# A new table of keys for the order of all steps in a convolution, Fourier and FFN kernel

## The chip, the cores and the metric

The kernel runs on one core of a Trainium2 chip, as one launch over 64 images. The metric is device time in microseconds: the median of three runs before is 7462.52 us (7462.07 to 7469.69). A core has five engines that run their own instruction queues: TensorE (PE; its weight loads are shown as PEld), VectorE (DVE), ScalarE (ACT), GpSimd (POOL) and SyncE (SP), which here issues DMAs.

## The reference

Two layers act on a tensor of 64 x 96 x 56 x 56 float32.

- Layer 0 is a convolution block: a 1x1 expansion from 96 to 192 channels with a batch norm and SiLU, a shift of four channel groups by one pixel each, a channel shuffle, a depthwise 3x3 with an identity branch and SiLU, a squeeze-and-excite gate, a 1x1 projection back to 96 channels, the residual, and SiLU.
- Layer 1 takes the 3136 pixels as tokens t of 96 channels.

```
t = t + attn(ln(t))   # ln: mean and variance over the 96 channels
t = t + ffn(ln(t))
# attn: h = relu(bn1(t @ w1.T)), 192 channels; X = fft over the 3136 tokens
#       xr = relu(Xr*rd - Xi*id + rb), xi = relu(Xi*rd + Xr*id + ib)
#       y = real(ifft(xr + i*xi)); bn2(y @ w2.T)
# ffn:  two linear layers 96 -> 384 -> 96, products rounded to fp8 (5 exponent bits),
#       sums and biases rounded to fp16, relu between
```

## The kernel before

**Work and tiles.** One image is one unit of work. It passes through 56 kinds of step, and each kind runs once to 21 times an image. A step is a small function with the arguments b (image) and i (which one), and it issues instructions to a single engine, apart from sp_ev, which also issues a DMA on SP. Names ending in _mm are TensorE's. The steps in the order of an image's data:

- x_in loads 8 rows of x (SP); ea_mm, eb_mm (PE, lines 383 and 400) expand; ea_ev, eb_ev (ACT) apply SiLU.
- dw_mm (L446) computes 128 of the 192 channels of the depthwise convolution on PE in two halves of three steps; lt (L466, L468) computes the other 64 on DVE. dw_ev (L456) and ls apply SiLU on ACT and give the sums for the gate.
- se1_mm (L478), se1_ev, se2_mm (L493), se2_ev, se2_th and se2_pw make the gate and fold it into the projection's weights.
- pj_mm (L532, L537), pj_add (DVE) and pj_ev (ACT) project, add x and write the tokens t.
- c_mm (L557), c_sq, c_v, c_pow (POOL) get the variance of each token; sp_v, sp_mm and sp_ev carry it to where w1 needs it: sp_ev writes a row of t by DMA.
- w1_mm (L626) and w1_ev; then the Fourier transform in two stages, f1_mm (L653) with f1_ev (L665, ACT) and f2_mm (L680, L690); f2_u (L705, ACT), f2_s (L721, L724, DVE), f2_r (L728, ACT) and f2_p (L734, DVE) do the complex scaling with its relu.
- w2_mm (L745, L757), w2_ev; the inverse transform i1_mm (L786), i1_ev, i2_mm (L808), i2_ev.
- n_mm, n_sq, n_v, n_pow, n_x, x_mm (L852), x_ev: the second layer norm, rounded to fp8.
- h_mm (L865), h_ev (L870, ACT), h_b (L875, DVE), h_q (L881, ACT): the first FFN layer, three h to one o; o_mm (L887), o_ev (L892), o_b (L897), o_f (L903, POOL) and o_st (SP): the second, the residual and the store.

**Order.** Nothing is reordered by a scheduler. A table PLAN gives each step a key relative to its image, PERIOD is added for each image, and all steps of all images are issued in the order of these sums:

```
with tc.manual_schedule():
    for _, b, k, i in sorted(
        (b * PERIOD + when, b, k, i)
        for b in range(NB)
        for k, step in enumerate(STEPS)
        for i, when in enumerate(PLAN[step.__name__])
    ):
        STEPS[k](b, i)
```

Each engine then has its part of this list as its own queue. Only the order of the keys matters; they are not times at which something happens. At equal sums the smaller b goes first, then the earlier kind of step. An image's keys reach from about -150 to +310, so in a repeat of one PERIOD the steps of several images interleave: with ea_mm to pj_mm of image b run c_mm to i2_mm of image b-1 (c_mm already of b towards the end), and n_mm to o_mm of image b-2. "Image" numbers in square brackets below are relative in this way.

**Buffers.** PSUM has two kinds here. Two buffers of 1024 columns (psa) are taken in turn by w1_mm, f1_mm, f2_mm, w2_mm, i1_mm and i2_mm: each waits until the step that reads the buffer two turns earlier is done. Four buffers of one bank (psb) serve all other matmuls; a step takes the one that was released first. Both waits, like those for data, are semaphores that the framework puts in. In SBUF the fp16 results of h have three buffers, and the fp8 results, the squares, the scaled spectrum and the outputs two each.

Of the kernel before, what the change touches and what calls it, by code (L numbers as in the profile page):

```python
# [38 lines left out]

PERIOD = 116.056
PLAN = {
    "x_in": (-142.751, -132.334, -138.890, -139.641, -151.208, -133.652, -137.370),
    "ea_mm": (-127.116, -124.446, -119.920, -94.498, -104.745, -112.167, -106.964),
    "ea_ev": (-125.252, -124.279, -119.721, -94.105, -94.974, -110.456, -105.960),
    "eb_mm": (-110.852, -109.364, -102.468, -94.672, -100.705),
    "eb_ev": (-109.889, -108.508, -98.175, -94.671, -100.704),
    "dw_mm": (-77.186, -75.415, -71.686, -59.708, -58.836, -58.630),
    "dw_ev": (-67.184, -68.088, -65.354, -62.005, -53.949, -53.481, -53.376, -53.432),  # L50
    "lt": (-93.236, -91.843, -90.397, -86.333, -83.176, -78.618, -75.060, -71.072, -58.358),
    "ls": (-56.957,),
    "se1_mm": (-52.674,),
    "se1_ev": (-52.590,),
    "se2_mm": (-49.560,),
    "se2_ev": (-47.764,),
    "se2_th": (-46.882,),
    "se2_pw": (-44.842,),
    "pj_mm": (-44.604, -44.263, -36.259, -33.499),
    "pj_add": (-41.623, -41.337, -40.573, -40.255, -32.468, -30.814, -32.509, -32.127),  # L60
    "pj_ev": (-41.036, -40.637, -40.429, -36.736, -30.334, -29.230, -31.146, -29.797),
# [1 line left out]
    "c_sq": (-23.198, -19.663, -17.391, -16.366, -11.963, -8.651, -8.871),
    "c_v": (-21.831, -17.939, -17.390, -11.021, -10.842, -8.366, -8.657),
    "c_pow": (-19.058, -12.292, -10.931, -8.952, -1.526, -3.948, -1.526),
    "sp_v": (-8.951, -1.525),
    "sp_mm": (-6.057, 0.802),
    "sp_ev": (-5.461, 1.113),
    "w1_mm": (1.423, -2.619, 3.588, 18.203, 8.943, 12.171, 13.999, 16.535),
    "w1_ev": (3.273, -0.045, 7.600, 20.920, 11.591, 14.999, 15.957, 19.212),  # L70
# [10 lines left out]
    "i1_ev": (86.931, 93.317, 99.344),
    "i2_mm": (102.107, 101.737, 110.644, 111.766),
    "i2_ev": (106.004, 107.037, 104.651, 104.395, 113.248, 110.645, 115.503, 113.393),
    "n_mm": (109.042, 108.523, 116.336, 120.505, 126.604, 126.539, 137.374),
    "n_sq": (109.105, 109.021, 116.337, 120.506, 127.174, 126.540, 137.375),
    "n_v": (109.642, 109.022, 116.338, 120.507, 127.975, 126.902, 138.122),
    "n_pow": (110.809, 110.170, 116.496, 122.658, 132.126, 129.135, 139.318),
    "n_x": (112.520, 110.693, 119.248, 123.053, 133.298, 130.929, 139.362),
    "x_mm": (113.125, 114.113, 121.321, 126.216, 135.244, 138.382, 142.002),
    "x_ev": (114.896, 115.709, 126.025, 126.217, 137.926, 142.365, 142.302),  # L90
# [1013 lines left out]
```

## Time and profile before

| | |
|---|---|
| median of three runs | 7462.52 us |
| profiled execution, time | 7463.64 us |
| profiled execution, span | 7461.9 us |
| granted TensorE clock | 0.991 |
| PE busy | 7176.9 us, 96% |
| PE weight loads busy | 5259.2 us, 70% |
| DVE busy | 4829.5 us, 65% |
| ACT busy | 4654.4 us, 62% |
| POOL busy | 1513.6 us, 20% |

The profile is of one execution: its span runs from the first to the last instruction, and the time is what the device reports for the same execution. Busy shares are averages. An idle stretch of an engine is listed with what ended it: "PE psa L745 <- DVE ue L724" means that a matmul of line 745, which writes psa, started when the VectorE instruction of line 724, which writes ue, was done. "issue" means that the profile shows nothing that the engine waited for. In a timeline each row is a run of like instructions: start, duration, engine, line, operation, out<-in, shapes and count.

### The profile page before, as it was taken

How to read it: one execution, taken by the hardware profiler on the slowest of the kernel's cores; microseconds unless marked ns; L12 is line 12 of the kernel's file. 1: busy time of each engine (PE TensorE's matmuls, PEld its weight loads, DVE VectorE, ACT ScalarE, POOL GpSimd, SP SyncE). 2: the span in 40 equal slices, each digit the busy share in tenths (PEclk: the TensorE clock that was granted, in tenths of full speed). 3: DMA queues.
4: the chain of work that ended last, by engine and by line, in shares of the span. 5: the costliest groups of instructions: out<-in, count | busy, mean ns of one | idle time of the engine just before them, and what ended most of it. 6: DMA issues, size and time to landing. Idle time of an engine off the chain costs nothing.

```text
span 7461.9 us, 383252 instructions
## 1 busy us (share of the span) xinstructions
PE 7176.9 (96%) x177666; PEld 5259.2 (70%) x177666; DVE 4829.5 (65%) x8795; ACT 4654.4 (62%) x9806; POOL 1513.6 (20%) x1360
## 2 busy tenths in 40 slices
PE   7999999999999999999999999999999999999997
PEld 4777777777777776777777777777777777777775
DVE  5666666666666666666666666666666666666664
ACT  3566666666665666656656666666566566665665
POOL 0221212212212122122121221221212212212112
PEclk9999999999999999999999999999999999999998
DMA  1010110110101101101011011010110110101100
GB/s 48 20 27 18 29 27 19 29 24 21 28 17 29 27 19 28 24 22 28 17 29 27 19 28 25 22 28 18 29 27 19 29 26 20 29 21 26 28 20 21
DMA packets 424331, 185.32 MB, mean 25 GB/s; under 512 B 378785, under 2 KB 422041, under 8 KB 422473
## 3 DMA queue, kind: packets, MB, share of 16 engines
q1 hardware_dynamic: 420970, 155.82, 9.1%
q8 instruction: 1392, 22.81, 1.3%
q10 hardware_dynamic: 1264, 3.48, 0.1%
q14 instruction: 209, 1.71, 0.1%
q0 software_dynamic: 496, 1.50, 0.1%
HBM read 82.80 MB, written 77.07 MB: 21 GB/s over the span
## 4 chain that ended last, share of the span: by engine, by line
PE 85%; ACT 6%; DVE 6%; issue 3%; DMA 0%; POOL 0%; POOLq 0%; SPq 0%; ACTq 0%
PE psa L653 9%; PE psa L626 9%; PE ps_d L446 8%; PE ps_eb L400 5%; PE ps_ea L383 5%; PE psa L808 5%; PE ps_pj L532 5%; PE ps_c L557 5%; PE psa L745 5%; PE ps_n L557 5%; PE psa L786 5%; PE psa L680 4%; PE ps_h L865 4%; PE ps_o L887 3%; DVE s L721 3%
## 5 line engine op out<-in xcount | busy, mean ns | idle before, releaser
L903 POOL TENSOR_TENSOR o<-t,o 112x448 f32<-112x448 f32 x448 | 613.9, 1370 | 3694.7 <-DMA out_dram<-o 1710.0
L446 PE MATMUL ps_d<-e_a,diag 32*32 32x392 f32 x36864 | 1033.2, 498 | 0.7 <-ACT d L456 0.7
L468 DVE SCALAR_TENSOR_TENSOR d_last<-e_b,taps,d_last 128x1568 f32<-128x1568 f32 x512 | 971.5, 1898 | 7.1
L875 DVE TENSOR_SCALAR y<-y,qb 128x448 f16<-128x448 f16 x1344 | 479.8, 365 | 683.9 <-ACT y L870 676.7
L568 DVE TENSOR_REDUCE v<-sq 112x4 f32<-112x384 f32 x896 | 491.3, 548 | 662.7 <-ACT sq L564 662.1
L446 PEld LDWEIGHTS ps_d<-e_a,diag 32*32 32x32 f32 x36864 | 673.6, 103 | 288.9 <-issue 40.0
L870 ACT CAST y<-ps_h 128x448 f16<-128x448 f32 x1344 | 697.2, 540 | 213.1 <-PE ps_h L865 209.5
L837 POOL TENSOR_TENSOR rs<-v,mhalf 112x4 f32<-112x4 f32 x448 | 490.3, 1099 | 1453.9 <-DVE v L569 1453.9
L881 ACT CAST h<-y 128x448 fp8e5<-128x448 f16 x1344 | 739.0, 571 | 3.0 <-DVE y L875 3.0
L653 PEld LDWEIGHTS psa<-f_tab,buf_h 128*56 128x56 f32 x24576 | 655.4, 131 | 77.8 <-DVE v L569 42.5
L626 PEld LDWEIGHTS psa<-w1c,t 112*64 112x64 f32 x14336 | 604.0, 137 | 141.4 <-DVE v L569 45.4
L653 PE MATMUL psa<-f_tab,buf_h 128*56 128x58 f32 x24576 | 688.9, 216 | 0.0
L626 PE MATMUL psa<-w1c,t 112*64 112x96 f32 x14336 | 676.2, 249 | 2.9 <-DMA t<-dev_t 1.4
L586 POOL TENSOR_TENSOR rs<-v,mhalf 112x4 f32<-112x4 f32 x448 | 447.6, 1012 | 763.6 <-DVE v L569 763.5
L638 DVE SCALAR_TENSOR_TENSOR buf_h<-psa,rs_full 128x768 f32<-128x768 f32 (+1 forms) x512 | 435.4, 851 | 137.4 <-PE psa L626 129.5
L543 DVE TENSOR_TENSOR ps_pj<-ps_pj,x 112x392 f32<-112x392 f32 x512 | 260.6, 566 | 404.5 <-PE ps_pj L537 392.3
L728 ACT ACTIVATE s<-s 128x896 f32<-128x896 f32 (+2 forms) x384 | 334.4, 887 | 288.8 <-DVE s L721 288.8
L388 ACT ACTIVATE e_a<-ps_ea 128x448 f32<-128x448 f32 x448 | 244.9, 547 | 412.5 <-PE ps_ea L383 412.5
L564 ACT ACTIVATE sq<-ps_n 112x384 f32<-112x384 f32 x448 | 214.1, 495 | 436.1 <-PE ps_n L557 434.8
L734 DVE SCALAR_TENSOR_TENSOR buf_h<-ue,s 128x448 f32<-128x448 f32 (+2 forms) x768 | 406.8, 580 | 109.4 <-ACT s L728 109.4
L549 ACT ACTIVATE t<-ps_pj,pjbn_b 112x392 f32<-112x392 f32 x512 | 281.4, 620 | 284.5 <-DVE ps_pj L543 284.5
L786 PE MATMUL psa<-inv_tab,buf_g 112*32 112x56 f32 x24576 | 350.5, 214 | 110.5 <-issue 108.8
(175 smaller groups left out, 13024.5 us busy)
## 6 DMA issues: line engine op xcount, KB each, us to landing
x<-in_x SPq DMA_DIRECT2D x896, 84.0 KB, 3.2
out_dram<-o SPq DMA_DIRECT2D x896, 84.0 KB, 2.2
l_tab<-in_tab_l ACTq DMA_DIRECT2D x1, 1624.0 KB
r_tab<-in_tab_r ACTq DMA_DIRECT2D x1, 1568.0 KB
t<-dev_t SPq DMA_DIRECT2D x64, 7.0 KB, 2.1
t<-dev_t SPq DMA_DIRECT2D x64, 5.2 KB
ex_row_p<-in_expand_row POOLq DMA_DIRECT2D x1, 336.0 KB, 4.5
s_p<-in_bn POOLq DMA_DIRECT2D x1, 288.0 KB, 3.8
```

The source lines that it names most:

```text
L446: nc.tensor.matmul(pss[r][j * 32 : j * 32 + 32], lhsT=diag[pr, tap, :], rhs=e_a[pr, r0 : r0 + PJ, dx : dx + HW], start=tap == 0, stop=tap ...
L468: nc.vector.scalar_tensor_tensor(d_last, win, w, d_last, ALU.mult, ALU.add)
L557: nc.tensor.matmul(cen[c0:c1, k, 0:C], lhsT=t_of(b)[:, n0 + c0 : n0 + c1], rhs=center, start=True, stop=True)
L568: nc.vector.tensor_reduce(v, sq, AX.X, ALU.add)
L626: nc.tensor.matmul(ps[hc * 64 : hc * 64 + 64, k, 0:C], lhsT=t[:, n0 : n0 + 64], rhs=w1c[:, hc * C : hc * C + C], start=True, stop=True,)
L653: nc.tensor.matmul(ps[r * 64 : r * 64 + HW, k, 0 : 2 * NK], lhsT=buf_h[:, n0 : n0 + HW], rhs=f_tab[:, r, :], start=True, stop=True,)
L786: nc.tensor.matmul(ps[p0 : p0 + 32, k, 0:HW], lhsT=u_v[:, oh * 48 + o, :], rhs=inv_tab[:, r, :], start=True, stop=True,)
L837: nc.gpsimd.tensor_tensor(rs, held.pop(("nv", b, g)), mhalf[0:CP, 0:4], ALU.pow)
L870: nc.scalar.copy(y16, held.pop(("h", b, i)))
L875: nc.vector.tensor_scalar(y16, y16, qb1[:, i % 3 : i % 3 + 1], 0.0, ALU.add, ALU.max)
L881: nc.scalar.copy(held["h8", b, j][:, m, :], held.pop(("y", b, i)), saturate=False)
L903: nc.gpsimd.tensor_tensor(o32, rows, o16, ALU.add)
```

## The change

PERIOD goes from 116.056 to 116.117, and every key in PLAN is replaced. No function changes, and each kind of step has as many entries as before, so the same instructions are issued in another order. The diff in its core (the other kinds of step have new keys in the same manner):

```diff
-PERIOD = 116.056
+PERIOD = 116.117
 PLAN = {
...
-    "dw_ev": (-67.184, -68.088, -65.354, -62.005, -53.949, -53.481, -53.376, -53.432),
+    "dw_ev": (-75.706, -75.706, -75.706, -75.705, -59.463, -58.046, -59.416, -59.640),
...
-    "c_mm": (-24.403, -20.404, -19.123, -17.297, -18.726, -9.644, -8.872),
+    "c_mm": (-24.700, -23.784, -22.561, -14.383, -22.138, -11.175, -15.521),
...
-    "f1_mm": (21.608, 26.248, 24.638, 31.810, 32.559, 32.004),
-    "f1_ev": (25.169, 25.895, 30.841, 28.844, 27.556, 26.595, 32.009, 32.411, 36.910, 36.732, 36.699, 35.929),
-    "f2_mm": (37.220, 36.994, 44.528, 54.196, 60.721, 63.959),
+    "f1_mm": (20.969, 24.138, 21.453, 27.916, 28.364, 29.033),
+    "f1_ev": (21.858, 21.828, 27.847, 26.717, 25.831, 26.083, 28.752, 28.380, 29.263, 29.263, 29.263, 29.263),
+    "f2_mm": (33.295, 29.847, 41.027, 45.394, 56.500, 57.570),
...
-    "f2_r": (44.699, 46.227, 59.499, 60.966, 71.228, 72.985),
+    "f2_r": (40.411, 40.237, 54.971, 56.273, 70.174, 75.875),
...
-    "i1_mm": (82.811, 83.639, 91.924),
+    "i1_mm": (81.789, 85.039, 89.118),
...
     "h_q": (
-        149.384, 151.139, 150.029, 159.215, 163.340, 163.159, 172.257, 183.329, 182.397, 187.024, 188.763, 189.403,
+        145.380, 145.381, 145.381, 154.154, 164.463, 155.147, 170.447, 186.761, 183.168, 187.741, 191.545, 191.927,
...
-    "o_mm": (153.028, 179.101, 192.712, 203.850, 207.474, 223.800, 230.382),
+    "o_mm": (145.964, 174.332, 192.700, 203.173, 205.203, 221.748, 227.957),
```

What the keys come to, in the queues (the number behind a name is i, the bracket the image relative to b):

| queue, stretch | before | after |
|---|---|---|
| PE, f1 | ea_mm3, f1_mm0[-1], x_mm5[-2], f1_mm2, x_mm6, f1_mm1, h_mm2, 0, 1, 4, f1_mm3, 5, 4, h_mm3, 5, o_mm0, f2_mm1, 0 | f1_mm0[-1], f1_mm2, x_mm5[-2], x_mm6, ea_mm3, f1_mm1, h_mm1, 2, 0, f1_mm3, 4, 5, h_mm5, 3, 4, o_mm0, f2_mm1, 0 |
| ACT, same | ... f1_ev6, 7, h_q0, 2, 1, f1_ev11, 10, 9, 8, h_ev3, 4, o_ev0, h_ev5, f2_u2 | ... f1_ev7, 6, f1_ev8, 9, 10, 11 (h_q0 before or behind these four), h_q1, h_q2, o_ev0, h_ev3, 5, 4, f2_u2 |
| PE, dw to w2 | dw_mm0 to 2, f2_mm2, h_mm6, 8, 7, f2_mm3, dw_mm3 to 5, f2_mm4, h_mm9, o_mm1, se1_mm, f2_mm5, h_mm10, se2_mm, h_mm12, 11, w2_mm0 | dw_mm0 to 2, f2_mm2, h_mm6, 8, f2_mm3, dw_mm3 to 5, f2_mm4, h_mm7, f2_mm5, h_mm9, se1_mm, h_mm11, o_mm1, h_mm10, se2_mm, h_mm12, w2_mm0 |
| ACT, same | f2_r2, f2_r3, dw_ev4, 5, 7, 6, f2_u8, 9, se1_ev, o_ev1, h_ev9, h_q8, f2_u10, 11 | f2_r2, ls, f2_r3, dw_ev7, 4, 6, f2_u8, h_ev7, f2_u9, dw_ev5, f2_u10, h_ev9, se1_ev, o_ev1, f2_u11 |
| PE, i1 to ea | i1_mm0, 1, h_mm15, 16, o_mm3, h_mm18, o_mm4, c_mm0, i1_mm2, h_mm20, c_mm1, 2, 4, h_mm19, c_mm3, h_mm17, i2_mm1, 0, ea_mm0, c_mm5, 6 | i1_mm0, h_mm15, i1_mm1, h_mm16, o_mm3, h_mm18, o_mm4, i1_mm2, h_mm20, c_mm0, 1, 2, 4, h_mm19, 17, i2_mm0, 1, ea_mm0, c_mm6, 3, 5 |

In the new table some sums of neighbouring images are equal to the third decimal, so that the rounding of the floating-point sum decides, image by image: f1_ev8 to 11 with h_q0 of the image before; f2_mm1 with o_mm0 of the image before; f2_r0 with dw_ev0 to 2 of the image after. Over 63 pairs of images, h_q0 goes ahead of f1_ev8 in 46 and behind f1_ev11 in 17; o_mm0 goes ahead of f2_mm1 in 56; f2_r0 goes ahead of dw_ev0 in 48 of 62. In the old table the order is the same in every image.

More of the change, by code (lines that the diff above doesn't have):

```diff
@@ L38 @@
 AT = {k: i for i, k in enumerate(ROWS)}
-PERIOD = 116.056
+PERIOD = 116.117
 PLAN = {
[L44 to L49, printed above, removed]
-    "dw_ev": (-67.184, -68.088, -65.354, -62.005, -53.949, -53.481, -53.376, -53.432),
[L51 to L61, printed above, removed]
-    "c_mm": (-24.403, -20.404, -19.123, -17.297, -18.726, -9.644, -8.872),
[L63 to L70, printed above, removed]
-    "f1_mm": (21.608, 26.248, 24.638, 31.810, 32.559, 32.004),
-    "f1_ev": (25.169, 25.895, 30.841, 28.844, 27.556, 26.595, 32.009, 32.411, 36.910, 36.732, 36.699, 35.929),
-    "f2_mm": (37.220, 36.994, 44.528, 54.196, 60.721, 63.959),
-    "f2_u": (39.991, 41.910, 38.664, 38.665, 56.185, 56.316, 56.071, 58.643, 62.858, 62.962, 66.464, 67.055),
-    "f2_s": (42.369, 43.646, 41.684, 42.524, 58.496, 59.412, 59.011, 59.603, 66.349, 66.780, 67.365, 69.133),
-    "f2_r": (44.699, 46.227, 59.499, 60.966, 71.228, 72.985),
-    "f2_p": (46.153, 47.154, 60.124, 60.967, 72.402, 74.345),
-    "w2_mm": (70.359, 71.061, 73.352, 79.154),
-    "w2_ev": (70.421, 73.788, 79.483, 82.773),
-    "i1_mm": (82.811, 83.639, 91.924),
[L81 to L90, printed above, removed]
@@ new lines @@
+    "x_in": (-133.111, -132.773, -131.474, -126.938, -117.060, -126.640, -137.775),
+    "ea_mm": (-131.687, -126.797, -120.627, -92.311, -105.349, -112.758, -107.738),
+    "ea_ev": (-127.703, -126.568, -120.284, -91.635, -103.549, -109.721, -102.230),
+    "eb_mm": (-111.410, -109.367, -98.933, -97.177, -101.764),
+    "eb_ev": (-110.762, -106.396, -95.891, -94.873, -101.599),
+    "dw_mm": (-78.108, -78.107, -75.867, -70.329, -59.642, -59.641),
+    "dw_ev": (-75.706, -75.706, -75.706, -75.705, -59.463, -58.046, -59.416, -59.640),
@@ new lines @@
+    "lt": (-92.955, -90.968, -88.993, -86.860, -82.955, -82.321, -81.541, -75.892, -71.251),
+    "ls": (-60.903,),
+    "se1_mm": (-57.938,),
+    "se1_ev": (-57.888,),
+    "se2_mm": (-56.697,),
+    "se2_ev": (-44.656,),
+    "se2_th": (-43.457,),
+    "se2_pw": (-43.229,),
+    "pj_mm": (-40.640, -40.639, -35.997, -35.413),
+    "pj_add": (-40.507, -40.614, -38.335, -39.834, -32.399, -35.412, -34.522, -33.993),
+    "pj_ev": (-39.774, -40.207, -37.034, -38.723, -31.989, -33.731, -32.329, -32.673),
@@ new lines @@
+    "c_mm": (-24.700, -23.784, -22.561, -14.383, -22.138, -11.175, -15.521),
+    "c_sq": (-24.185, -21.848, -18.168, -10.701, -14.456, -10.542, -8.794),
+    "c_v": (-21.469, -20.843, -17.507, -10.700, -9.213, -10.541, -7.866),
+    "c_pow": (-20.976, -14.114, -11.436, -10.125, -7.354, -1.787, -7.539),
+    "sp_v": (-9.982, -1.742),
+    "sp_mm": (-8.702, -0.435),
+    "sp_ev": (-7.854, 1.311),
+    "w1_mm": (2.648, -1.000, 1.600, 17.538, 5.650, 11.771, 6.870, 15.639),
+    "w1_ev": (4.072, 1.505, 4.502, 20.857, 10.411, 16.325, 8.154, 19.551),
@@ new lines @@
+    "f1_mm": (20.969, 24.138, 21.453, 27.916, 28.364, 29.033),
+    "f1_ev": (21.858, 21.828, 27.847, 26.717, 25.831, 26.083, 28.752, 28.380, 29.263, 29.263, 29.263, 29.263),
+    "f2_mm": (33.295, 29.847, 41.027, 45.394, 56.500, 57.570),
+    "f2_u": (37.806, 38.239, 37.253, 37.254, 47.543, 47.915, 53.216, 53.472, 57.620, 58.056, 58.087, 63.805),
+    "f2_s": (38.343, 39.785, 37.254, 38.759, 50.829, 51.789, 55.756, 56.240, 63.563, 69.537, 69.567, 70.963),
+    "f2_r": (40.411, 40.237, 54.971, 56.273, 70.174, 75.875),
@@ new lines @@
+    "f2_p": (43.219, 42.386, 56.571, 58.035, 74.554, 77.033),
+    "w2_mm": (72.802, 74.980, 75.721, 77.872),
+    "w2_ev": (75.445, 75.316, 79.813, 80.196),
+    "i1_mm": (81.789, 85.039, 89.118),
+    "i1_ev": (86.942, 88.114, 91.615),
+    "i2_mm": (96.615, 97.501, 108.909, 110.467),
+    "i2_ev": (103.068, 99.512, 104.959, 100.215, 113.634, 109.805, 110.838, 115.117),
+    "n_mm": (107.474, 106.827, 114.824, 119.532, 126.545, 125.920, 134.645),
+    "n_sq": (108.311, 107.582, 116.698, 122.219, 128.365, 126.889, 137.073),
@@ L91 @@
+    "n_v": (108.426, 109.421, 117.364, 123.378, 128.526, 130.097, 138.126),
+    "n_pow": (109.423, 113.370, 121.043, 123.871, 132.933, 130.894, 138.290),
+    "n_x": (110.125, 114.965, 121.044, 123.904, 133.290, 131.209, 138.789),
+    "x_mm": (111.995, 115.392, 122.347, 124.126, 134.017, 138.495, 138.925),
+    "x_ev": (115.233, 116.998, 123.693, 124.499, 136.619, 140.304, 139.993),
     "h_mm": (
-        144.408, 144.539, 142.955, 151.653, 146.123, 151.741, 165.593, 167.081, 167.021, 179.037, 181.701, 184.163,
@@ L93 @@
-        183.315, 191.401, 194.122, 202.572, 203.025, 214.978, 205.482, 214.132, 209.133,
+        143.259, 140.773, 140.872, 145.171, 145.960, 145.167, 157.293, 173.481, 159.830, 174.290, 174.763, 174.298,
+        186.033, 192.521, 193.972, 198.856, 201.575, 212.518, 204.525, 211.767, 205.889,
     ),
     "h_ev": (
-        146.457, 147.163, 146.728, 153.132, 153.156, 154.262, 168.465, 171.753, 169.119, 180.037, 185.733, 184.280,
-        187.040, 192.972, 195.243, 203.531, 205.107, 216.376, 208.878, 222.205, 212.052,
+        143.683, 143.468, 144.490, 149.091, 152.967, 149.902, 157.294, 174.088, 159.831, 174.291, 189.186, 184.650,
@@ L98 @@
+        191.107, 193.642, 195.656, 199.010, 206.699, 214.894, 205.152, 219.957, 206.891,
     ),
     "h_b": (
-        146.899, 148.834, 148.614, 154.505, 157.941, 159.836, 170.515, 176.287, 174.097, 185.812, 187.639, 185.918,
-        191.781, 195.030, 198.861, 204.123, 206.545, 220.428, 209.152, 226.370, 218.475,
+        145.178, 145.133, 145.199, 152.176, 155.868, 152.927, 166.624, 177.329, 177.764, 186.132, 189.564, 191.018,
+        196.492, 195.308, 198.866, 204.592, 210.596, 217.381, 209.776, 220.326, 210.913,
@@ L102 @@
     ),
     "h_q": (
-        149.384, 151.139, 150.029, 159.215, 163.340, 163.159, 172.257, 183.329, 182.397, 187.024, 188.763, 189.403,
-        196.328, 198.478, 200.406, 208.755, 210.002, 221.499, 217.314, 229.791, 224.579,
-    ),
-    "o_mm": (153.028, 179.101, 192.712, 203.850, 207.474, 223.800, 230.382),
-    "o_ev": (154.015, 179.621, 193.552, 207.958, 209.955, 223.824, 232.254),
-    "o_b": (167.276, 193.254, 201.506, 209.696, 210.604, 235.187, 237.499),
-    "o_f": (171.766, 199.519, 206.356, 219.602, 231.322, 259.139, 253.186),
@@ L111 @@
-    "o_st": (197.792, 218.616, 214.282, 229.895, 257.122, 313.688, 263.438),
+        145.380, 145.381, 145.381, 154.154, 164.463, 155.147, 170.447, 186.761, 183.168, 187.741, 191.545, 191.927,
+        196.946, 197.196, 199.151, 205.684, 212.535, 221.177, 213.581, 223.306, 225.989,
+    ),
+    "o_mm": (145.964, 174.332, 192.700, 203.173, 205.203, 221.748, 227.957),
+    "o_ev": (146.282, 174.675, 193.958, 207.173, 206.559, 222.908, 228.670),
+    "o_b": (152.607, 199.269, 195.548, 217.158, 208.570, 253.275, 240.658),
@@ L112 @@
+    "o_f": (163.411, 201.284, 201.572, 219.752, 222.497, 256.796, 270.096),
+    "o_st": (177.420, 204.543, 205.736, 241.601, 226.275, 276.627, 300.625),
 }
```

## The prediction

> **What bounds the kernel now.** I read the page first, then the waits of TensorE (PE), then the timeline of image 30 where PE meets another engine.
>
> From the page: engines' busy time, the chain that ended last, and the queue that fetches instructions (packets, MB, share of the DMA engines).
>
> ```profile
> span 7461.9 us, 383252 instructions
> PE 7176.9 (96%) x177666; PEld 5259.2 (70%) x177666; DVE 4829.5 (65%) x8795; ACT 4654.4 (62%) x9806; POOL 1513.6 (20%) x1360
> ...
> q8 instruction: 1392, 22.81, 1.3%
> ...
> PE 85%; ACT 6%; DVE 6%; issue 3%; DMA 0%; POOL 0%; POOLq 0%; SPq 0%; ACTq 0%
> ```
>
> PE is the bound, and 85% of the chain is its own work. All the change can win or lose is time in which PE stands still. The waits of PE show where that is (total us, times, longest):
>
> ```profile
> PE psa L786 <- issue: 108.8, 68, 2.2
> PE psa L745 <- DVE ue L724: 50.8, 64, 1.7
> ...
> PE ps_o L887 <- ACT h L881: 4.8, 4, 2.8
> ```
>
> Two places recur in every image. At i1_mm (L786) PE waits for nothing that the profile shows; at the first w2_mm (L745) it waits for VectorE's f2_s. o_mm (L887) hardly ever waits for ScalarE's h_q (L881). To see how the stretches of a period add up I took start-to-start distances on PE, means over images 6 to 57:
>
> - ea_mm0 to f1_mm0 36.67 us, the same in every image to 0.04
> - f1_mm0 to f2_mm2 24.24
> - f2_mm2 to w2_mm0 18.25
> - w2_mm0 to i1_mm0 18.17, the same in every image
> - i1_mm0 to the next ea_mm0 17.35, from 15.85 to 19.90
>
> They sum to 114.68 us an image. Three stretches run without jitter: every wait in them is covered. So the prediction asks, stretch by stretch, whether the new order keeps that cover.
>
> The place that matters most is the end of f1. Timeline of image 30 (start, duration, engine, line, count):
>
> ```profile
> 3457.99 3.83 PE L653 MATMUL psa<-f_tab,buf_h 128*56 128x58 f32 x141
> ...
> 3459.44 1.51 ACT L881 CAST h<-y 128x448 fp8e5<-128x448 f16 x3
> 3460.84 2.02 ACT L665 COPY buf_g<-psa 128x464 f32<-128x464 f32 x4
> 3461.75 0.55 PE L865 MATMUL ps_h<-xq,q 96*128 96x448 fp8e5 x2
> ...
> 3462.14 0.73 PE L887 MATMUL ps_o<-h,q 128*112 128x448 fp8e5 x3
> 3462.80 0.60 PE L690 MATMUL psa<-l_tab,buf_g 128*64 128x112 f32 x8
> ```
>
> ACT runs h_q0, 2, 1 (L881, x3) while PE still runs the last f1_mm, and only then the four last f1_ev (L665). When PE reaches o_mm0 (L887) all three h_q have been done for 1.00 us.
>
> The second place is w2_mm0:
>
> ```profile
> 3488.28 1.26 ACT L705 ACTIVATE ue<-psa,fb 128x392 f32<-128x392 f32 x2
> ...
> 3491.42 0.62 DVE L724 SCALAR_TENSOR_TENSOR ue<-psa,fb,ue 128x392 f32<-128x392 f32 x1
> ...
> 3492.10 0.54 PE L745 MATMUL psa<-w2a,buf_h 128*64 128x96 f32 x7 [0.52 <-DVE ue L724]
> ```
>
> w2_mm0 writes the shared buffer that f2_mm4 filled, so it waits until f2_s9 (L724) has read it: h_mm11 to w2_mm0 takes 1.33 us, where a step after a lone h_mm otherwise starts 0.47 later.
>
> [...] the steps of PE, ACT, DVE and POOL stand in the order of their keys in all 23,744 places. So a step that waits holds all behind it. [...] 256 PE instructions run in 1.55 us and PE then pauses 1.5 to 2.3 us, until 2.3 to 2.9 us after the packet's start.
>
> **The change part by part.** No instruction is added or removed, so busy times stay (PE 7177 us). Only what stands before what changes. Durations below: spacing on ACT of f1_ev 0.44, h_q 0.47, dw_ev 0.56, f2_u 0.60, h_ev 0.43 us; h_q lasts 0.57, f1_ev 0.55.
>
> *End of f1 (the largest term).* The new ACT order is f1_ev8, 9, 10, 11, then h_q1, h_q2; PE's is f1_mm5, three h_mm, o_mm0, f2_mm1. f1_ev10 reads f1_mm5, so h_q2 now stands behind PE's last f1_mm, and o_mm0 needs h_q2. From the end E of f1_mm5: f1_ev10 at E+0.04, f1_ev11 at 0.48, h_q1 at 0.92, h_q2 from 1.39 to 1.96. PE has the h_mm at E-0.07, -0.06 and 0.13, o_mm0 from 0.32, and would start f2_mm1 at 1.17. It now issues o_mm0's third matmul at about 2.02 and f2_mm1 0.47 later, at 2.49: 1.32 us lost. Three sets of keys are equal in the new plan to the third decimal across images, so rounding of b*PERIOD decides: in 45 of 63 images h_q0 goes before f1_ev8 (1.3 us lost); in 11 it goes behind f1_ev11 as well (0.47 more: 1.8); in 7 f2_mm1 goes before o_mm0 and waits only for f1_ev11, until 1.08 against 0.60 (0.5). Sum 45x1.3 + 11x1.8 + 7x0.5 = 82 us. Queued behind o_mm0 on PE are f2_mm1, f2_mm0 and all of dw_mm; ACT's h_ev and f2_u wait with them, so nothing else gets late. Bounds: 0.5 if all images had the last form (31 us), 1.8 if all had the second (112).
>
> *f2_mm2 to w2_mm0.* h_mm7 leaves the place before f2_mm3 (0.19 saved) and comes back after f2_mm4; f2_mm5 goes ahead of h_mm9, o_mm1, se1_mm. Unhindered, f2_mm4 to w2_mm0 is 1.49 + 0.47 + 1.11 + 0.29 + 0.54 + 0.01 + 0.58 + 0.29 + 0.56 + 0.47 = 5.81. ACT from f2_mm4's start: dw_ev7 at -0.14, dw_ev4 0.42, dw_ev6 0.98, f2_u8 1.61, h_ev7 2.17, f2_u9 2.60, dw_ev5 3.16 with its sum at 3.84. se1_mm stands at 3.36 and its sixth sum comes at 3.84: 0.2 lost, and 0.1 more behind h_ev9 and o_ev1. f2_s8 starts at 3.35, f2_s9 ends 5.83; PE is there at 6.12, so w2_mm0's wait is gone. 6.12 against 6.21, with the 0.19: -0.28 us an image, -17 over 62 images. In 14 images dw_ev0 to 2 stand before f2_r0 (a tie again); h_ev8 then ends 0.3 after PE wants dw_mm3: +4. Bounds: -0.9 (the whole wait gone) to +0.3.
>
> *i1_mm0 to ea_mm0.* c_mm0 goes behind i1_mm2, h_mm15 between i1_mm0 and i1_mm1, c_mm3 behind ea_mm0. Up to i1_mm2's end PE needs 786 instructions instead of 818, at some 3.7 us a block (the packets here start 3.5 to 4.2 us apart): 0.46 us less. But c_mm0's 0.62 comes after: +0.16. The c_mm now run in a row (0.62 a step instead of 0.80): -0.13. I take 0. Bounds: -1.5 (half of the 3.1 us that this stretch loses over the 14.28 its steps take unhindered) to +0.7.
>
> *The rest.* ea_mm0 to f1_mm0 and w2_mm0 to i1_mm0 cost nothing while their covers hold; the thinnest new ones, worked out in the same way, are w1_mm3 behind w1_ev5 (0.3), pj_mm2 behind h_ev14 (0.24), x_mm1 behind n_x1 (0.7) and sp_mm0. c_mm3 is now computed 5 us later, and c_sq3, c_v3, c_pow3, sp_v0 follow it; sp_mm0 finds sp_v0 done 0.35 before. If that cover goes, PE loses what is missing. SP: the x_in go behind o_st1 and o_st2 of the image two before, issued some 4.8 us after i1_mm0, and land 7 us before ea_mm0; the two dev rows stand behind x_in5 and x_in4, 3.5 us or more before w1_mm needs them. POOL keeps its 21 steps; o_f3 stands before c_pow2 and is ready. Filling and draining (130 us before the first f1_mm0, 129 after the last) keep their chains: 0, give or take 3.
>
> Sum: 82 - 17 + 4 + 0 = +69 us. The profiled execution took 7463.6 (span 7461.9 and 1.7 around it), 1.1 over the median of 7462.5. 7462.5 + 69 = 7531.
>
> **Rivals.** A: *the wait is repaid.* w2_mm0's wait goes without a new one at se1_mm, -55 instead of -13, and the c_mm in a row give 10: 7462.5 + 82 - 55 - 10 = 7480. For it: 50.8 us stand in the waits; against: dw_ev5's late sum. B, the other side: *the instruction pauses shrink.* h_mm15 splits the i1_mm, and the loads of x[...] start later. It decides from 1.1 us an image on, since 69/63 must be made good; at half of the pauses, 1.5 us x 63 = 95: 7531 - 95 = 7436. For it: 108.8 us at L786 alone; against: a block still takes 2.3 us or more and i1_mm still eats one in 1.55. C: *late c_mm3 breaks the cover of sp_mm0*, or another thin one goes, 0.5 to 1 us more: 7531 + 47 = 7578. D: the order is the same in effect. That can't be, as h_q1 and 2 stand behind f1_ev11 in all images.
>
> **Numbers.** Forecast 0.52 (7508 to 7563), A 0.20, B 0.12, C 0.16. 0.2% (15 us) is about what a measurement tells from no change. Faster: B and a little of A, 0.13; within 15 us: part of A, 0.06; slower 0.81. The range leaves out B and the top of C: 7465 to 7580.
>
> **What would show it.** Right: PE ps_o <- ACT h grows from 4.8 to some 80 us; L745 <- DVE falls under 10; f1_mm0 to f2_mm2 grows by 1.3 us; the i1 stretch stays near 17.3. Wrong: o_mm0 starting without a wait, or the i1 stretch under 16.2 us.

## The result, and the profile after

The changed kernel takes 7579.62 us (median of four runs, 7576.16 to 7582.7); the kernel before took 7465.1 us on the same chip. The ratio is 1.0153, with a 95% interval from 1.0135 to 1.0170: 114 us slower. The forecast was 7531 us. The measured time lies outside the range of the likeliest case (7508 to 7563) and 0.4 us inside the upper end of the whole range (7465 to 7580).

The page of the changed kernel, the same parts as shown of before (engines' busy time, the chain that ended last):

```profile
span 7574.2 us, 383167 instructions
PE 7213.3 (95%) x177666; PEld 5265.1 (70%) x177666; DVE 4938.2 (65%) x8795; ACT 4679.5 (62%) x9806; POOL 1527.3 (20%) x1360
...
PE 84%; DVE 7%; ACT 6%; issue 3%; DMA 0%; POOL 0%; ACTq 0%; POOLq 0%; SPq 0%; DVEq 0%
```

PE issues the same 177,666 matmuls. The span grew by 112.3 us. The waits of PE say what it stood still for (total us, times, longest):

```profile
PE psa L786 <- issue: 75.8, 90, 2.2
PE ps_dev L600 <- DVE dev L593: 57.3, 64, 2.6
PE ps_o L887 <- ACT h L881: 45.3, 61, 1.5
...
PE ps_se L478 <- ACT d L456: 34.6, 66, 0.9
PE ps_c L557 <- issue: 26.0, 31, 1.7
PE psa L745 <- DVE gate L506: 12.1, 55, 0.2
...
PE psa L745 <- DVE ue L724: 1.9, 2, 1.3
```

Three things are read from it. The forecast wait of o_mm0 for h_q (L887 <- L881) is there, in 61 places. The old wait of w2_mm0 for f2_s9 (L745 <- L724, 50.8 us before) is gone, as forecast. And a wait stands there that the sum did not hold: sp_mm0 (L600) waits for sp_v0 (L593), in all 64 images.

The same start-to-start distances on PE as in the prediction, means over images 6 to 57, in us:

| stretch | before | after | difference | forecast |
|---|---|---|---|---|
| ea_mm0 to f1_mm0 | 36.67 | 37.66 | +0.99 | 0 |
| f1_mm0 to f2_mm2 | 24.24 | 26.01 | +1.77 | +1.3 |
| f2_mm2 to w2_mm0 | 18.25 | 18.13 | -0.12 | -0.28 |
| w2_mm0 to i1_mm0 | 18.17 | 18.62 | +0.45 | 0 |
| i1_mm0 to the next ea_mm0 | 17.35 | 15.78 | -1.57 | 0 |

Two steps changed stretches. c_mm3 left the last one for the first and took its 0.66 us along; ea_mm3 left the first for the second (0.61 us: without a wait f1_mm0 to f2_mm1 takes 13.67 in the new order and 13.06 in the old). Without these moves the differences are +0.94 (0.92 of it at sp_mm0), +1.16, -0.12, +0.45 and -0.91. They sum to 1.52 us, and 63 repeats make 96 us. The rest of the 112 is outside these means: filling is 5.8 us longer (the first f1_mm0 at 135.9 instead of 130.1), draining 2.1, and the images at both ends some 8.

Part of the last two differences is no wait. The trace records the clock granted to PE, and in it stand spells at half clock: 24 in the profiled execution before, 18 after. Of these 21 and 15 last 3.41 us; the other three of each trace last 6.8 to 51.8 us and stand near the ends of the span. Over images 6 to 57, a spell of 3.41 us falls between i1_mm0 and ea_mm0 in 15 images before and in none after, and between w2_mm0 and i1_mm0 in none before and in 7 after. Two windows of 3.4 us in the changed kernel, from the start of w2_mm0 in image 28 (half clock) and in image 29 (full clock); in brackets the instructions of PE, PEld, DVE, ACT and POOL, then the clock (PEclk) and the DMA engines' share and GB/s:

```profile
3428.60:3432.00 3.40, 3.40 (x49) 3.16 (x52) 2.69 (x7) 3.37 (x9) 0.00 (x0) 0.50 0.02 5
3545.30:3548.70 3.40, 3.18 (x84) 2.86 (x85) 2.65 (x7) 3.37 (x9) 0.00 (x0) 1.00 0.03 7
```

At half clock PE starts 49 matmuls where it otherwise starts 84. Without the images that hold such a spell, i1_mm0 to ea_mm0 takes 16.94 us before (17.35 with them) and 15.78 after, and w2_mm0 to i1_mm0 takes 18.45 after (18.62 with them). So some 0.41 of the -0.91 us and 0.17 of the +0.45 us go with the clock. What sets the place of these spells, no run here shows.

### The profile page after: what moved, and what is told of

Read it like the earlier page. It is cut to its first block, busy times and chain, and to the rows that moved or that the text cites. A ratio compares the mean times of both kernels' runs of the same rounds, so it can differ in the third digit from the quotient of the medians.

```text
span 7574.2 us, 383167 instructions
## 1 busy us (share of the span) xinstructions
PE 7213.3 (95%) x177666; PEld 5265.1 (70%) x177666; DVE 4938.2 (65%) x8795; ACT 4679.5 (62%) x9806; POOL 1527.3 (20%) x1360
## 3 DMA queue, kind: packets, MB, share of 16 engines
q8 instruction: 1392, 22.81, 1.3%
## 4 chain that ended last, share of the span: by engine, by line
PE 84%; DVE 7%; ACT 6%; issue 3%; DMA 0%; POOL 0%; ACTq 0%; POOLq 0%; SPq 0%; DVEq 0%
PE ps_d L446 13%; PE psa L653 9%; PE psa L626 9%; PE ps_eb L400 5%; PE psa L808 5%; PE ps_pj L532 5%; PE psa L786 4%; PE psa L680 4%; PE ps_n L557 4%; PE ps_ea L383 4%; PE psa L745 4%; PE ps_h L865 3%; PE ps_o L887 3%; PE ps_pj L537 3%; PE ps_c L557 3%
## 5 line engine op out<-in xcount | busy, mean ns | idle before, releaser
L903 POOL TENSOR_TENSOR o<-t,o 112x448 f32<-112x448 f32 x448 | 629.0, 1416 | 3889.4 <-DVE o L897 3773.6
L468 DVE SCALAR_TENSOR_TENSOR d_last<-e_b,taps,d_last 128x1568 f32<-128x1568 f32 x512 | 1003.3, 1960 | 11.5
L881 ACT CAST h<-y 128x448 fp8e5<-128x448 f16 x1344 | 743.8, 579 | 7.1 <-DVE y L875 7.0
L837 POOL TENSOR_TENSOR rs<-v,mhalf 112x4 f32<-112x4 f32 x448 | 447.0, 1007 | 1351.6 <-DVE v L569 1351.6
L626 PE MATMUL psa<-w1c,t 112*64 112x96 f32 x14336 | 691.8, 250 | 5.7 <-DVE buf_h L638 3.9
L586 POOL TENSOR_TENSOR rs<-v,mhalf 112x4 f32<-112x4 f32 x448 | 451.5, 1016 | 769.4 <-DVE v L569 415.9
L665 ACT COPY buf_g<-psa 128x464 f32<-128x464 f32 x768 | 389.7, 552 | 176.4 <-PE psa L653 176.4
L859 ACT CAST xq<-ps_x 96x448 fp8e5<-96x448 f32 x448 | 230.4, 528 | 403.8 <-PE ps_x L852 403.8
L413 ACT ACTIVATE e_b<-ps_eb 128x392 f32<-128x392 f32 x256 | 127.5, 498 | 549.5 <-PE ps_eb L400 549.5
L786 PE MATMUL psa<-inv_tab,buf_g 112*32 112x56 f32 x24576 | 369.9, 214 | 77.1 <-issue 75.8
L786 PEld LDWEIGHTS psa<-inv_tab,buf_g 112*32 112x32 f32 x24576 | 327.0, 110 | 162.9 <-issue 149.2
```

The costliest lines, as they stand in the source:

```text
L468: nc.vector.scalar_tensor_tensor(d_last, win, w, d_last, ALU.mult, ALU.add)
L586: nc.gpsimd.tensor_tensor(rs[:, js], v[:, js], mhalf[0:CP, 0:4], ALU.pow)
L626: nc.tensor.matmul(ps[hc * 64 : hc * 64 + 64, k, 0:C], lhsT=t[:, n0 : n0 + 64], rhs=w1c[:, hc * C : hc * C + C], start=True, stop=True,)
L786: nc.tensor.matmul(ps[p0 : p0 + 32, k, 0:HW], lhsT=u_v[:, oh * 48 + o, :], rhs=inv_tab[:, r, :], start=True, stop=True,)
L881: nc.scalar.copy(held["h8", b, j][:, m, :], held.pop(("y", b, i)), saturate=False)
L903: nc.gpsimd.tensor_tensor(o32, rows, o16, ALU.add)
```

## Experiments

Chips differ a little (the kernel before took 7465 to 7483 us on those used), so each run is compared by its ratio to the kernel before on its own chip; 0.001 is 7.5 us. The ratios' intervals reach 0.0007 to 0.0019 to either side, so the difference of two ratios is good to some 17 us where each has 0.0016.

**o_f4 away from sp_v0.** POOL's add o_f4 runs ahead of o_f3, nothing else moves.

```diff
-    "o_f": (163.411, 201.284, 201.572, 219.752, 222.497, 256.796, 270.096),
+    "o_f": (163.411, 201.284, 201.572, 219.752, 219.417, 256.796, 270.096),
```

> The changed kernel, with one step of POOL moved: o_f4 goes ahead of o_f3, so that it no longer runs beside sp_v0. Two readings of why sp_mm0 waits 0.92 us an image in the changed kernel (n_mm1 to sp_mm0 takes 1.72 us; after n_mm2 the same step takes 0.80). Theory, the add itself is held up: sp_v0 on DVE lasts 1.27 us while o_f4 runs on POOL (both start within 0.07 us), and 0.17 us where no POOL step runs beside it, as sp_v1 here and sp_v0 in the kernel before. Then sp_v0 falls to 0.17, the wait goes, and 0.92 x 62 = 57 us come back. Rival, c_mm3 is computed too late (the prediction's rival C): sp_v0 starts no earlier when o_f4 moves, and 0 us come back.

Ratio 1.0078 (1.0063 to 1.0094) against 1.0153: 56 us came back. First the place in the changed kernel, from its timeline of image 30:

```profile
3699.70 1.01 POOL L586 TENSOR_TENSOR rs<-v,mhalf 112x4 f32<-112x4 f32 x1 [0.48 <-DVE v L569]
...
3700.68 1.30 POOL L903 TENSOR_TENSOR o<-t,o 112x448 f32<-112x448 f32 x1
3700.74 1.27 DVE L593 TENSOR_TENSOR dev<-v,rs 112x16 f32<-112x16 f32 x1
...
3702.16 0.35 PE L600 MATMUL ps_dev<-eye,dev 112*16 112x112 f32 x2 [0.87 <-DVE dev L593]
```

c_pow3 (L586) ends at 3700.71, sp_v0 starts at once, and then a multiplication of 112x16 numbers takes 1.27 us: it ends 0.03 after the POOL add beside it. The durations of line 593 (min/median/max ns), in the kernel before, in the changed one and in this run:

```profile
L593 DVE TENSOR_TENSOR dev<-v,rs x128: 161/172/1270, 105.5 to 7314.7; 112x16 f32<-112x16 f32 x64, 112x12 f32<-112x12 f32 x64
```

```profile
L593 DVE TENSOR_TENSOR dev<-v,rs x128: 157/174/1281, 108.1 to 7422.0; 112x16 f32<-112x16 f32 x64, 112x12 f32<-112x12 f32 x64
```

```profile
L593 DVE TENSOR_TENSOR dev<-v,rs x128: 170/174/177, 107.3 to 7385.6; 112x16 f32<-112x16 f32 x64, 112x12 f32<-112x12 f32 x64
```

With o_f4 gone from beside it no execution is slow, and ea_mm0 to f1_mm0 falls from 37.66 to 36.73 us, though c_mm3 is as late as ever. So rival C named the right place for the wrong reason. The traces of before and after part the two durations without exception: in each, 62 executions of line 593 take 1.26 to 1.28 us, all beside an o_f (L903) that started 0.06 to 0.07 us earlier, and they end 0.02 to 0.04 us after it; the other 66 take 0.16 to 0.18 us, and no POOL instruction runs beside any of them. By what means the add holds the multiplication up, they don't show.

**h_q ahead of the last f1_ev.**

```diff
     "h_q": (
-        145.380, 145.381, 145.381, 154.154, 164.463, 155.147, 170.447, 186.761, 183.168, 187.741, 191.545, 191.927,
+        145.210, 145.220, 145.230, 154.154, 164.463, 155.147, 170.447, 186.761, 183.168, 187.741, 191.545, 191.927,
```

> The changed kernel with h_q0, h_q1 and h_q2 ahead of f1_ev8 to f1_ev11 on ACT in all images, nothing else moved. Theory, o_mm0 waits for h_q1 and h_q2 alone: o_mm0 to f2_mm1 falls from 1.98 us (2.44 in some images) to 0.85, f1_mm0 to f2_mm1 from 14.76 to 13.67, and 1.09 x 63 = 69 us come back. Rival, the cost only moves: f2_mm1 then waits for f1_ev11, which ends 0.5 us later on ACT; then some 40 us come back.

Ratio 1.0065 (1.0046 to 1.0084): 66 us came back. o_mm0 to f2_mm1 is 0.85 us again, the stretch f1_mm0 to f2_mm1 went from 14.76 to 13.67, and of PE's wait for h_q only the filling is left (the 7 images in which f2_mm1 goes ahead of o_mm0 are as they were):

```profile
PE ps_o L887 <- ACT h L881: 4.4, 5, 1.5
```

**The same step alone, in the kernel before.** h_q1 and h_q2 go behind the last f1_ev.

```diff
     "h_q": (
-        149.384, 151.139, 150.029, 159.215, 163.340, 163.159, 172.257, 183.329, 182.397, 187.024, 188.763, 189.403,
+        149.384, 152.976, 152.986, 159.215, 163.340, 163.159, 172.257, 183.329, 182.397, 187.024, 188.763, 189.403,
```

> The kernel before with the end of f1 alone: h_q1 and h_q2 go behind the four last f1_ev on ACT, h_q0 stays ahead of them; nothing else moves. This is the prediction's largest step done alone. Theory: o_mm0 waits for h_q2, some 1.1 to 1.3 us in every image, that is 70 to 82 us (the undone step gave 66). Rival: PE uses the time to fetch instructions that it pauses for later, and the cost is 50 us or less.

Ratio 1.0089 (1.0073 to 1.0104): 66 us, from 54 to 78. In the trace f1_mm0 to f2_mm1 grows from 13.06 to 14.38 us in every image, which is 82 us over 63 images. The stretch at i1 is 0.14 us shorter in this trace (17.21), 9 us, which leaves 73. That is no sign of the rival: PE's waits without a releaser at L786 and L557 are 127.4 us here and 127.4 in the kernel before. Half-clock spells fall into this stretch in 11 images here and in 15 before.

**dw_ev5's sum earlier.** f2_u9 and dw_ev5 go ahead of h_ev7 on ACT.

```diff
-    "dw_ev": (-75.706, -75.706, -75.706, -75.705, -59.463, -58.046, -59.416, -59.640),
+    "dw_ev": (-75.706, -75.706, -75.706, -75.705, -59.463, -58.467, -59.416, -59.640),
...
-    "f2_u": (37.806, 38.239, 37.253, 37.254, 47.543, 47.915, 53.216, 53.472, 57.620, 58.056, 58.087, 63.805),
+    "f2_u": (37.806, 38.239, 37.253, 37.254, 47.543, 47.915, 53.216, 53.472, 57.620, 57.630, 58.087, 63.805),
...
     "h_b": (
-        145.178, 145.133, 145.199, 152.176, 155.868, 152.927, 166.624, 177.329, 177.764, 186.132, 189.564, 191.018,
+        145.178, 145.133, 145.199, 152.176, 155.868, 152.927, 166.624, 185.662, 177.764, 186.132, 189.564, 191.018,
```

> The changed kernel with f2_u9 and dw_ev5 ahead of h_ev7 on ACT (and h_b7 behind f2_s9 on DVE, so that f2_s8 isn't held by it). Theory, se1_mm waits for dw_ev5's sum and for that alone: the sum comes 0.36 us earlier, se1_mm to h_mm11 falls from 1.21 to 0.85, and 0.36 x 63 = 23 us come back; w2_mm1's wait of 0.26 for f2_s11 stays. Rival, the wait only moves: h_ev7 ends 1.2 us later and gives its buffer back later, so that o_mm1 or h_mm10 waits for it and 0 us or less come back.

Ratio 1.0099 (1.0082 to 1.0116): 40 us came back, give or take some 18, so not told apart from the 23 expected; in the trace the two stretches from f2_mm2 to i1_mm0 lose 0.49 us, 31 us, of which 3 are half-clock spells (4 images instead of 7). se1_mm to h_mm11 fell from 1.21 to 0.78 us, so the wait for the sum was the cause. Both readings missed something. h_mm10 now starts 0.06 us after h_ev9's end, and h_mm10 to se2_mm takes 0.73 instead of 0.47: the rival's wait for a buffer took 0.26 back, as far as the times show it. But w2_mm1's wait of 0.26 us went too. o_mm1 comes earlier, so o_ev1 and f2_u11 behind it on ACT do, and f2_s10 and f2_s11 with them. That wait was a follower of se1_mm's, not one of its own.

**The order of PE around i1 alone, in the kernel before.**

```diff
-    "c_mm": (-24.403, -20.404, -19.123, -17.297, -18.726, -9.644, -8.872),
+    "c_mm": (-22.556, -20.404, -19.123, -17.297, -18.726, -9.644, -8.872),
...
-        183.315, 191.401, 194.122, 202.572, 203.025, 214.978, 205.482, 214.132, 209.133,
+        183.315, 191.401, 194.122, 199.256, 203.025, 214.978, 205.482, 214.132, 209.133,
```

> The kernel before, with the new order of PE around i1 alone: h_mm15 between i1_mm0 and i1_mm1, c_mm0 behind i1_mm2 and h_mm20 (pj_add6 and pj_ev6 a little earlier, so that h_mm15 has a buffer; c_sq0 and c_v0 follow c_mm0). The loads of x stay where they were and c_mm3 too. Theory, the order of PE makes the pauses shorter: the stretch i1_mm0 to ea_mm0 falls from 17.35 by 0.95 us, and the time by 0.95 x 63 = 60 us. Rival, the later loads of x do it: 0 us, and 17.2 to 17.5 us in the stretch. The prediction itself said 0 for the order.

Ratio 0.9980 (0.9973 to 0.9986): 15 us faster, a quarter of what was to be explained. The stretch is 17.26 us. But the order did not make the pauses shorter. PE's waits without a releaser around i1, in the kernel before (L786 had 108.8) and in this run:

```profile
PE ps_c L557 <- issue: 18.6, 20, 1.9
```

```profile
PE psa L786 <- issue: 106.5, 114, 2.8
...
PE ps_c L557 <- issue: 21.0, 24, 1.7
```

Both add up to the same, 127.4 and 127.5 us. What differs is the granted clock: 0.993 on average over the 20 executions here, 0.990 over the 23 of the kernel before on this chip, where 0.001 less of clock goes with some 5 us more. That is enough for the whole 15 us. In images without a half-clock spell, i1_mm0 to ea_mm0 takes 17.13 us here and 16.94 in the kernel before. Whether the order changed the clock, and how, isn't shown.

**Later loads of x alone, and both.**

```diff
-    "x_in": (-142.751, -132.334, -138.890, -139.641, -151.208, -133.652, -137.370),
+    "x_in": (-129.112, -128.912, -128.112, -125.612, -119.112, -125.512, -129.312),
```

> The kernel before with the loads of x later on SP alone: all seven x_in stand behind o_st2 and o_st1, as in the changed kernel, and so start some 3.8 us after i1_mm0, where six of them used to start about 2 us after it. The order of all compute steps is that of before. Theory, [...] later loads shorten the pauses at i1: i1_mm0 to ea_mm0 falls from 17.35 to some 16.6 us and the time by 0.75 x 63 = 47 us. Rival, the time of the loads doesn't matter (what the changed kernel won there came from c_mm3 and the order of PE): 0 us. Second rival: the last loads come too late for ea_mm0, and the time grows.

Ratio 0.9971 (0.9958 to 0.9983): 22 us faster; i1_mm0 to ea_mm0 fell from 17.35 to 16.77 us, and from 16.94 to 16.58 in images without a half-clock spell (5 images hold one instead of 15). PE's waits without a releaser at L786 and L557 fell from 127.4 to 116.0 us. The compute steps have their old order, so the time of the loads matters, but by 11 us of pauses where the theory had 47; the clock is higher again (0.993 against 0.991). By what means the loads act on the pauses is not shown.

> The kernel before with both: the loads of x later on SP and the new order of PE around i1 (h_mm15 between i1_mm0 and i1_mm1, c_mm0 behind i1_mm2 and h_mm20); c_mm3 stays. Theory: the two add up to what the changed kernel won in this stretch, some 0.95 us an image, 60 us; with the order alone at 15 us, the loads give 45. Rival, what was won came with c_mm3 leaving the stretch or with other places of the blocks: 15 us, as the order gave alone.

Ratio 0.9963 (0.9950 to 0.9976): 28 us, and 16.76 us in the stretch. PE's waits without a releaser are 106.0 us: 21 less than in the kernel before, 10 less than with the loads alone. The sum of the two times, 37 us, is not told apart from 28.

**The loads of x early again, in the changed kernel.**

```diff
-    "x_in": (-133.111, -132.773, -131.474, -126.938, -117.060, -126.640, -137.775),
+    "x_in": (-145.834, -132.774, -145.634, -145.734, -151.334, -133.774, -145.534),
...
-    "o_st": (177.420, 204.543, 205.736, 241.601, 226.275, 276.627, 300.625),
+    "o_st": (177.420, 218.617, 205.736, 241.601, 226.275, 276.627, 300.625),
```

> The changed kernel with the loads of x as early on SP as before (x_in4 first, then 0, 3, 2, 6 behind o_st0 and ahead of o_st2, and o_st1 behind x_in1). Theory, the loads lengthen the pauses: i1_mm0 to the next ea_mm0 grows from 15.8 by some 0.7 us, the time by 45 us. Rival, their time doesn't matter: 0 us.

Ratio 1.0179 (1.0164 to 1.0194) against 1.0153: some 20 us slower, give or take 17, with 15.99 instead of 15.78 us in the stretch. PE's waits without a releaser grew from 101.8 to 111.4 us, 10 us: the mirror of the 11 that later loads took from the kernel before.

**c_mm3 out of the stretch as well, in the kernel before.** To the loads and the order of i1 this adds:

```diff
-    "c_mm": (-22.556, -20.404, -19.123, -17.297, -18.726, -9.644, -8.872),
+    "c_mm": (-22.556, -20.404, -19.123, -9.300, -18.726, -9.644, -8.872),
```

> The kernel before with the later loads of x, the new order of PE around i1, and c_mm3 out of the stretch as well (behind ea_mm0 and c_mm5, with c_sq3, c_v3 and sp_v0 after it). The first two gave 28 us together. Theory: c_mm3 leaving was the third part of what the changed kernel won here; PE asks for 32 instructions less in the crowded stretch, and some 20 us more are won (ratio about 0.993). Rival: the place of c_mm3 doesn't matter: 0.996 again. Second rival: its chain comes late at sp_mm0 here too, and the ratio goes over 1.

Ratio 0.9976 (0.9967 to 0.9986): nothing more was won, and filling took 9 us longer. Without c_mm3's own 0.66 us the stretch is 16.30, which answers to 16.96 with it. There is a new wait in it: i2_mm1 waits for i1_ev2 (L797):

```profile
PE psa L808 <- ACT buf_h L797: 14.3, 53, 1.1
```

So c_mm3's place is not the third part: PE's waits without a releaser are 113.2 us, not fewer than the 106.0 without this move. Of the 0.91 us that the changed kernel wins around i1, 0.41 are half-clock spells that went elsewhere; PE's pauses fell by 26 us (127.4 to 101.8), 0.40 an image, and the loads together with the order of PE gave 21 in the kernel before. Where the rest is from stays open.

**The three mended waits together.** The changed kernel with three edits from above: those of o_f4, of h_q0 to 2, and of f2_u9 and dw_ev5.

> The changed kernel with the three moves of the first runs together: o_f4 ahead of o_f3 on POOL, h_q0 to 2 ahead of f1_ev8 to 11 on ACT, f2_u9 and dw_ev5 ahead of h_ev7 on ACT. Theory, the three waits are separate and add up: 56 + 66 + 40 = 162 us less than the changed kernel, some 47 us under the kernel before (ratio about 0.994). Rival, PE that waits less runs into the pauses for instructions earlier and gives part of it back (in the profiles of the single moves the stretches from w2_mm0 on grew by 0.2 to 0.4 us an image): then it ends 0 to 30 us under the kernel before.

Ratio 0.9946 (0.9931 to 0.9961), 7422.77 us: some 155 us less than the changed kernel and 40 under the kernel before. The waits are separate. Nothing was given back: the stretch at i1 is 15.77 us, as in the changed kernel (15.78). More than half of what looked like it in two of the single moves were half-clock spells between w2_mm0 and i1_mm0, in 14 and 16 images there, 7 in the changed kernel and 5 here.

**Three of the loads of x ahead of i1.** On top of the mended kernel:

```diff
-    "x_in": (-133.111, -132.773, -131.474, -126.938, -117.060, -126.640, -137.775),
+    "x_in": (-153.734, -153.634, -153.534, -126.938, -117.060, -126.640, -137.775),
```

> The changed kernel with the three mended waits, and with x_in0, x_in1 and x_in2 moved ahead of i1 on SP (behind o_st6; their rows are free once pj_add0 to 3 have read them), so that four loads instead of seven run beside i1. Theory, any load beside the instruction blocks lengthens the pauses: i1_mm0 to ea_mm0 falls from 15.77 by 0.2 us or more, and the ratio from 0.9946 to 0.993 or under. Rival: the loads now meet the blocks of w2 and pj instead, and the time stays or grows.

The rows are not free, contrary to what is said there: pj_add4 and pj_add6 still read rows 14 to 27, and the three loads write rows 0 to 23, so in this run rows 14 to 23 get the next image's x as their residual. The work takes as long as before. Ratio 0.9934 (0.9918 to 0.9951), not told apart from 0.9946, and 15.88 us in the stretch: no gain.

**pj_mm3 between i1_mm0 and i1_mm1.** On top of the mended kernel, in the main (h_b14, h_mm15, h_ev15 and two pj_add follow):

```diff
-    "pj_mm": (-40.640, -40.639, -35.997, -35.413),
+    "pj_mm": (-40.640, -40.639, -35.997, -34.217),
...
-    "i1_ev": (86.942, 88.114, 91.615),
+    "i1_ev": (82.200, 88.114, 91.615),
```

> The changed kernel with the three mended waits, and pj_mm3 between i1_mm0 and i1_mm1 on PE instead of ahead of both (h_mm15 goes behind i1_mm1, since it needs a buffer that pj_ev5 gives back; h_b14, i1_ev0 and h_ev15 change places on DVE and ACT to suit). pj_mm3 keeps PE busy for 3.25 us with few instructions. Theory, the pauses at i1 come from two steps in a row that use up a block in 1.55 us each while a new one takes 3.3 us or more: with pj_mm3 between them a block comes in meanwhile, and of some 1.6 us of pauses an image about 1 goes, less 0.2 that i1_mm0 waits for w2_ev3: 50 us, and the ratio falls from 0.9946 to about 0.988. Rival, the whole stretch is short of blocks, and the pause only moves to i1_mm2 and the c_mm: 0.994 to 0.998.

7355.4 us, ratio 0.9842 (0.9825 to 0.9859): 78 us less than the mended kernel and 118 less than the kernel before. PE's waits without a releaser at i1, in this run:

```profile
PE ps_c L557 <- issue: 12.0, 24, 0.9
...
PE psa L786 <- issue: 2.2, 3, 1.3
```

They were 27.1 and 74.6 us in the mended kernel. PE's timeline of image 30:

```profile
3568.70 1.59 PE L532 MATMUL ps_pj<-d,pw 32*112 32x392 f32 x16
3570.22 1.78 PE L786 MATMUL psa<-inv_tab,buf_g 112*32 112x56 f32 x128
3571.93 1.58 PE L532 MATMUL ps_pj<-d,pw 32*112 32x392 f32 x16
3573.45 1.57 PE L537 MATMUL ps_pj<-d_last,pw 64*112 64x392 f32 x8
3574.95 1.78 PE L786 MATMUL psa<-inv_tab,buf_g 112*32 112x56 f32 x128
```

i1_mm asks for 128 matmuls and as many weight loads in 1.7 us, pj_mm3 for 24 and 24 in 3.0. With the two kinds in turn PE pauses at L786 for 2.2 us in the whole run. The stretch from w2_mm0 to ea_mm0 falls from 34.11 to 32.91 us, 76 us in 63 repeats; 0.20 us of it, 13 us, come back from ea_mm0 to f1_mm0 (36.73 to 36.93). The rival, that the pause only moves on, falls. What the pauses go with, the traces of before and after show: in each the instruction queue (q8) moves 1392 packets of 16.4 KB while PE runs 355,332 matmuls and weight loads, one packet (a "block" in the recorded texts) to 255 of them. All 88 pauses without a releaser at L786 and L557 before end 2.2 to 3.2 us after such a packet starts, and all 121 after end 2.2 to 3.3 us after it; of all PE instructions on these two lines 22% start 2.2 to 3.2 us after one. This run fits the reading that a pause depends on how many instructions the steps that stand in a row take per microsecond. Other ways to space them weren't tried.

## Why the prediction was right or wrong

The sign and the mechanism of the largest term were right. The total came out 45 us low because four terms were off, two of them by nearly as much as the largest term, with opposite signs.

- **End of f1: +82 forecast, 66 measured** by undoing it in the 56 images that wait (69 in the trace). The timeline of image 30 in the changed kernel shows the chain as written, with all times from f1_mm5's end at 3629.74:

```profile
3629.80 0.99 ACT L665 COPY buf_g<-psa 128x464 f32<-128x464 f32 x2 [0.66 <-PE psa L653]
...
3630.26 0.35 PE L887 MATMUL ps_o<-h,q 128*112 128x448 fp8e5 x1
3630.67 1.04 ACT L881 CAST h<-y 128x448 fp8e5<-128x448 f16 x2
3631.31 0.81 PE L887 MATMUL ps_o<-h,q 128*112 128x448 fp8e5 x2 [0.69 <-ACT h L881]
...
3632.05 0.41 PE L690 MATMUL psa<-l_tab,buf_g 128*64 128x112 f32 x3
```

  f1_ev10 and 11, then h_q1 and h_q2, and PE inside o_mm0 until h_q2 is done at 1.98 (forecast 1.96). The mis-sized term is "f2_mm1 0.47 later": f2_mm1 starts at 2.31, some 0.3 after the third matmul. So the usual form costs 1.1 us instead of 1.32. The forms that rounding decides were 0.8 (7 images) and 1.6 (11), where 0.5 and 1.8 had been given.
- **f2_mm2 to w2_mm0: -17 forecast.** w2_mm0's wait went, as forecast. The step that failed is "0.2 lost" at se1_mm: 0.67 us were lost there. From f2_mm4's start, ACT stood 0.2 later than forecast all along this row, so that dw_ev5 was done at 4.06 instead of 3.84, and PE came to se1_mm at 3.19 instead of 3.36. The next late thing, w2_mm1, was not in the sum at all: o_mm1 behind se1_mm holds o_ev1, which holds f2_u11 on ACT, and w2_mm1 starts 0.42 us late on average. Of that 0.26 is this chain; in 7 of 52 images w2_mm0 runs at half clock and takes 1.1 to 1.3 us longer. Together the two stretches from f2_mm2 to i1_mm0 grew by 0.33 us, 21 us in place of -17.
- **i1_mm0 to ea_mm0: 0 forecast, -0.91 us, about -57.** The step that failed is "I take 0". It counted PE's instructions at some 3.7 us for 256, the author's estimate from the spacing of the packets, and left the loads of x out, though rival B named them: moving these alone is worth 11 us of pauses one way and 10 the other. The order alone took nothing from the pauses (127.4 and 127.5 us), and on top of the loads 10. The half-clock spells, 0.41 of the 0.91 us, were in nobody's sum. Rival B had the sign and the place, but the pauses gave it under half of the size; at 0.91 it stayed just under the 1.1 that it needed to decide. A stretch under 16.2 us was named as a sign of being wrong, and it came: 15.78, or 16.44 with c_mm3 counted in.
- **The rest: 0 forecast, +57 at sp_mm0.** "sp_mm0 finds sp_v0 done 0.35 before" took sp_v0 at 0.17 us. At the place where it now stands o_f4 runs beside it, and it takes 1.27: a cover of 0.35 turns into a wait of 0.9. The row of line 593 in the kernel before already had the second value, for sp_v1 beside the same o_f4. Lack of jitter could not tell whether a wait is covered: ea_mm0 to f1_mm0 stays between 37.64 and 37.70 us in the changed kernel, with the 0.92 in it. And of the three stretches called free of jitter two are; f1_mm0 to f2_mm2 runs from 24.16 to 24.65 us. PE's busy time, taken to stay at 7177 us, reads 7213.3 with the same matmuls; the runs don't settle why.
- **Filling and draining: 0 give or take 3, measured +8.** Its parts weren't tried.

The likeliest case was too small, and rival C's 7578 us was met almost exactly, by luck in part: its place was right, its cause was not, and the gain around i1, which was not in its sum, paid for the losses at se1_mm and w2_mm1, for the ends, and for what the clock added at w2_mm0.

## What to carry to other kernels

When a step is moved, price it at its new place: look at the longest duration of its line as well as the median (here 1.27 and 0.17 us), and ask which instruction of another engine will run beside it. A short cover is only as good as the longest of these. Where an engine pauses between steps as dense as i1_mm (256 PE instructions in 1.7 us), try a step with few and long instructions (pj_mm3, 48 in 3.0 us) between two of them; here that was worth more (78 us) than any single wait on another engine that the new order made. And look at the granted clock of the executions before an order gets the credit for 15 us in 7465.

## What was not expected of the hardware

- A DVE multiplication of 112x16 numbers takes 0.17 us with no POOL instruction beside it and 1.27 us beside a POOL add of 112x448, and then ends 0.03 us after that add.
- PE's pauses at i1, 74.6 us in 90 places, fell to 2.2 us in 3 places by one step of 48 PE instructions put between two of 256.
- PE's pauses at L786 and L557 go with the time of the loads of x: later loads took them from 127.4 to 116.0 us in the kernel before, earlier ones from 101.8 to 111.4 in the changed one.
- Spells of 3.41 us at half clock stand in the traces, 21 before and 15 after, and their place differs between the two orders. Between w2_mm0 and i1_mm0 none of 52 images holds one in the six traces with the order of before, and 4 to 16 do in the eight with the new one; in the changed kernel w2_mm0 to w2_mm1 then takes 3.6 to 3.9 us instead of 2.57.
